# Linear attention and a mixture of experts on one core: the first chunk's scores and the list entries get other places in the issue order

## The chip, the cores and the metric

The kernel runs on one core of a Trainium2 chip. The metric is the device time of one execution in microseconds; three runs are known of the kernel before. A profile of one further execution shows what each engine did. The engines go by short names: PE is TensorE's matmuls and PEld its weight loads, DVE is VectorE, ACT is ScalarE, POOL is GpSimd, SP is the engine that here only issues transfers.

## What is computed

Input `x` is 2048 tokens of 512 numbers. The block is a pre-norm layer of two parts, all in float32:

```
x = x + attention(layernorm(x))
x = x + experts(layernorm(x))

attention: q = x Wq (16 heads of 128), k = x Wk, v = x Wv (4 heads of 128, each shared by 4 q heads)
           rotary embedding on q and k, then f(t) = elu(t) + 1
           state_t = state_{t-1} + k_t v_t^T,  z_t = z_{t-1} + k_t
           out_t = (q_t state_t) / (q_t z_t + 1e-6);  out Wo

experts:   scores = softmax(x Wc) over 64; the best 8 of scores + bias
           32 of the 64 are experts with weights (silu(x Wg) * (x Wu)) Wd; the others add no output
           of their own but scale the token's sum; at most 256 tokens to an expert
```

The recurrence over tokens is computed in chunks of 128: inside a chunk as masked scores times values, across chunks through the state.

## The kernel before

The tokens go in four blocks (`sb`, 512 tokens), each of four chunks (`c`, 128 tokens); there are four key heads (`g`), each with four query heads (`R`). The loop over blocks is at L552, over heads at L556, over chunks at L571.

For each block, `norm_block` (L267) normalises the tokens and puts them, transposed, into `xT`, of which there is one buffer. `values` (L288) makes `va`, the values of a chunk for all heads. `project` (L313) makes `kT` and `qT` of one head: one PSUM tile `pk` and four `pq` (tag `pj`, two buffers), each of four float32 matmuls that the profile shows as two instructions each, followed by `rope_feature` (L300), which is six operations on VectorE and one exponential on ScalarE per tile. `kT` and `qT` have two buffers, so a head's projection can write its result only when the attention of the head before last has ended.

`attend` (L332) handles one chunk of one head: the scores `psc` (L338; PSUM pool `p_sc`, one buffer), the masked scores `at` on VectorE (L340, two buffers), the products `po` of the masked scores with the values (L347) and of the queries with the state (L350), the denominators `den` (L353, L354), the divided rows `osb` on ScalarE (L356), the new state (L359 to L369), and the transposed result `oT` (L372, L373).

In the order of the program the projection of the next head (L560), or for the last head the next block's norm and first projection (L562, L563), stands ahead of the attention of the present one (L572).

After the last head's chunk `c` the result of chunk `c - 1` goes through `output` (L375): 16 products with `wo` into `px`, the residual sum `x1` (L387), and the second layer norm, whose power (the reciprocal square root) runs on GpSimd (`lnr`, L264) and whose normalised row is `xw` (L395). The function `rstd_of` keeps the power traced last as `rstd_of.last`. Chunks wait in the list `waiting` for `route` (L398), which scores the experts, takes the best 8, and makes `ai`, the places of a chunk's tokens in the lists of the experts. `list_further` (L197) then issues eight indirect transfers on GpSimd (L200), one for each of a token's eight choices, into `slots` in DRAM. `route_and_list` (L487) is the two together.

In the last block, `rows_so_far` (L514) reads the first rows of the lists back through SP (`idx_8b`, L518) and reduces them on VectorE to `low` (L520); `rows_in_groups` (L525) makes of them the index `idx_m_f`, which is used at L656, ahead of the first gathers of the experts' phase. Chunk 14's routing is issued between the two halves of chunk 15's output, and its list behind chunk 15's power.

The instructions are not issued in the order of the program text alone. A planner at compile time gives every instruction the priority of its place in the text and orders each engine's queue by priority among those that it reckons ready, with buffers given out as they come free. On the chip each queue then runs in that fixed order. `tc.issue_after(ins)` makes the instructions in its block that run on the engine of `ins` come behind `ins` in that engine's queue. The dependences between tiles are kept by semaphores.

The experts' phase (L829 on) gathers rows, runs the experts in groups of four, and adds to the output by indirect transfers; the change leaves it as it is.

Of the kernel before, what the change touches and what calls it, by code (L numbers as in the profile page):

```python
# [18 lines left out]
P = 128  # L19
# [48 lines left out]
def linattn_moe(  # L68
# [128 lines left out]
    def list_further(ch, ai, ks=range(TOPK)):  # L197

        for k in ks:
            one = nc.gpsimd.indirect_dma_start(  # L200
                out=slots[k][:, :],
                out_offset=bass.IndirectOffsetOnAxis(ap=ai[:, k : k + 1], axis=0),
                in_=tok[:, ch : ch + 1],
                in_offset=None,
                bounds_check=NS - 1,
                oob_is_err=False,
            )
        return one


    with ExitStack() as ph:
# [47 lines left out]
        def rstd_of(var, n, name):  # L259

            v = sml.tile([P, n], F32, tag=f"lnv{n}", name=f"lnv_{name}")
            nc.vector.tensor_scalar(v, var, 1e-5, None, ALU.add)
            r = sml.tile([P, n], F32, tag=f"lnr{n}", name=f"lnr_{name}")
            rstd_of.last = nc.gpsimd.tensor_tensor(r, v, mhalf[:, :n], ALU.pow)  # L264
            return r
# [63 lines left out]

        state = [None] * G  # L330

        def attend(sb, g, c, proj, va, oT):  # L332

            kT, qT = proj
            n = f"{sb}_{g}_{c}"
            cc = ts(c, P)
            psc = p_sc.tile([P, R, P], F32, tag="sc", name=f"psc_{n}")
            nc.tensor.matmul(psc, lhsT=kT[:, cc], rhs=qT[:, :, cc], start=True, stop=True)  # L338
            at = tmp.tile([P, R, P], F32, tag="at", name=f"at_{n}")
            nc.vector.tensor_tensor(at, psc, causal.unsqueeze(1).to_broadcast([P, R, P]), ALU.mult)  # L340
            old = state[g]
            osb = tmp.tile([P, R, HD], F32, tag="osb", name=f"osb_{n}")
            for j in range(R // 2):
                po = p_o.tile([P, 2, HD + 1], F32, tag="o", name=f"po_{n}_{j}")
                for i in range(2):
                    r = 2 * j + i
                    nc.tensor.matmul(po[:, i, :], lhsT=at[:, r, :], rhs=va[:, g, :],  # L347
                                     start=True, stop=(old is None))
                    if old is not None:
                        nc.tensor.matmul(po[:, i, :], lhsT=qT[:, r, cc], rhs=old,  # L350
                                         start=False, stop=True)
                den = sml.tile([P, 2], F32, tag="den", name=f"den_{n}_{j}")
                nc.vector.tensor_scalar(den, po[:, :, HD], 1e-6, None, ALU.add)  # L353
                nc.vector.reciprocal(den, den)  # L354
                for i in range(2):
                    nc.scalar.mul(osb[:, 2 * j + i, :], po[:, i, :HD], den[:, i : i + 1])  # L356
            if sb < NSB - 1 or c < NC - 1:
                pk = p_tr.tile([P, HD], F32, tag="tr", name=f"pk_{n}")
                nc.tensor.transpose(pk, kT[:, cc], ident)  # L359
                kk = tmp.tile([P, HD], F32, tag="kk", name=f"kk_{n}")  # L360
                nc.scalar.copy(kk, pk)
                pst = p_ms.tile([P, HD + 1], F32, tag="ms", name=f"pst_{n}")
                nc.tensor.matmul(pst, lhsT=kk, rhs=va[:, g, :], start=True, stop=True)  # L363
                new = stp.tile([P, HD + 1], F32, tag=f"st{g}", name=f"state_{n}")
                if old is None:
                    nc.vector.tensor_copy(new, pst)  # L366
                else:
                    nc.vector.tensor_tensor(new, pst, old, ALU.add)
                state[g] = new  # L369
            pt = p_tr.tile([P, R, P], F32, tag="tr", name=f"pot_{n}")  # L370
            for r in range(R):
                nc.tensor.transpose(pt[:, r, :], osb[:, r, :], ident)  # L372
            nc.vector.tensor_copy(oT[:, :, cc], pt)  # L373

        def output(sb, c, oTs, between=None):  # L375

            ch = sb * NC + c
            xs, _, _ = blocks[sb]
            px = p_pj.tile([P, D], F32, tag="pj", name=f"px_{ch}")
            for h in range(H):  # L380
                if between is not None and h == H // 2:
                    between()
                output.last = nc.tensor.matmul(px, lhsT=oTs[h // R][:, h % R, ts(c, P)],  # L383
                                                  rhs=wo[h // R][:, h % R, :],
                                                  start=(h == 0), stop=(h == H - 1))
            x1 = tmp.tile([P, D], F32, tag="row", name=f"x1_{ch}")
            nc.vector.tensor_tensor(x1, px, xs[:, c, :], ALU.add)  # L387
            tc.chain_iter_dep("out", nc.scalar.dma_start(out=out[ts(ch, P), :], in_=x1).ins)
            st = sml.tile([P, 6], F32, tag="st", name=f"st2_{ch}")
            nc.vector.bn_stats(st, x1)  # L390
            mv = sml.tile([P, 2], F32, tag="mv", name=f"mv2_{ch}")
            nc.vector.bn_aggr(mv, st)
            rstd = rstd_of(mv[:, 1:2], 1, f"2_{ch}")
            xw = tmp.tile([P, XW], F32, tag="xw", name=f"xw_{ch}")
            nc.vector.tensor_scalar(xw[:, :D], x1, mv[:, 0:1], rstd, ALU.subtract, ALU.mult)  # L395
            return xw
# [90 lines left out]
        def route_and_list(ch, xw):  # L487
            list_further(*route(ch, xw))
# [60 lines left out]
        projs = {(0, 0): project(0, 0, xTs[0])}  # L549
        oTs = {}  # L550
        waiting = []
        for sb in range(NSB):  # L552
            last = sb == NSB - 1
            if not last:
                blocks[sb + 1] = load_block(sb + 1)
            for g in range(G):  # L556
                if g == 0:
                    vas = [values(sb, c, xTs[sb]) for c in range(NC)]
                if g + 1 < G:
                    projs[sb, g + 1] = project(sb, g + 1, xTs[sb])  # L560
                elif not last:
                    xTs[sb + 1] = norm_block(sb + 1)  # L562
                    projs[sb + 1, 0] = project(sb + 1, 0, xTs[sb + 1])  # L563
                if last and g == 1:
                    rank_e = place()
                if last and g == G - 1:
                    for i in range(2):
                        load_pair(i)
                oT = otp.tile([P, R, SB], F32, tag="oT", name=f"oT_{sb}_{g}")
                oTs[sb, g] = oT  # L570
                for c in range(NC):  # L571
                    attend(sb, g, c, projs[sb, g], vas[c], oT)  # L572
                    if g == G - 1:
                        if c != 1 and waiting:
                            route_and_list(*waiting.pop(0))
                        if c >= 1:
                            waiting.append((sb * NC + c - 1,
                                            output(sb, c - 1, [oTs[sb, i] for i in range(G)])))
            listed = []
            if last:  # L580
                low_f = rows_so_far()
            xw = output(sb, NC - 1, [oTs[sb, i] for i in range(G)],
                        (lambda: listed.append(route(*waiting.pop(0)))) if last else None)
            with tc.issue_after(rstd_of.last.ins):
                for one in listed:
                    list_further(*one)
            while waiting:
                route_and_list(*waiting.pop(0))
            if last:
                with tc.issue_after(output.last.ins):  # L590
                    rows_in_groups(low_f)
                route(sb * NC + NC - 1, xw)
            else:
                waiting.append((sb * NC + NC - 1, xw))
# [43 lines left out]
    _, words = nc.values_load_multi_w_load_instructions(  # L638
        flags[0:1, :], min_val=0, max_val=65535,
        skip_runtime_bounds_check_because="a sum of 16 different powers of two below 2^16",  # L640
    )
# [189 lines left out]
    one = list_further(S // P - 1, ai_last, range(HEAD))  # L831
    with tc.issue_after(one.ins):
        for q in range(EARLY):
            g = gather(xg_b[q], idx_b[:, q : q + 1], XR)
# [3 lines left out]
    with tc.issue_after(g.ins):  # L838
        one = list_further(S // P - 1, ai_last, range(HEAD, TOPK))
# [23 lines left out]
    def gather_first(q):  # L863
        gather(xg_o[q % 2], column(Q * q, 0), S)
        return gather(xg_t[q % 2], column(Q * q, 1), S)
# [39 lines left out]
    for q in range(NQ):  # L905
        g = gather_first(q + 1) if q + 1 < NQ else None
# [63 lines left out]
```

## Time and profile before

| what | value |
|---|---|
| median of three runs (lowest, highest) | 1131.75 us (1129.96, 1133.35) |
| the profiled execution: time, span | 1135.13 us, 1133.4 us |
| mean granted TensorE clock in the span | 0.964 |
| 0 to 100 us: TensorE, VectorE busy | 89.3, 70.8 us |
| 100 to 200 us | 93.2, 66.7 |
| 200 to 300 us | 98.2, 52.4 |
| 300 to 400 us | 93.1, 77.5 |
| 400 to 500 us | 98.6, 46.4 |
| 500 to 600 us | 93.4, 72.5 |
| 600 to 700 us | 98.1, 42.9 |
| 700 to 800 us | 98.6, 79.1 |
| 800 to 900 us | 83.6, 44.2 |
| 900 to 1000 us | 77.8, 26.1 |
| 1000 to 1134 us | 102.0, 28.5 |

The blocks of attention begin near 20, 244, 463 and 682 us; the stretches with fewer transfers and more VectorE work are the projections and the attention of the heads, those with TensorE near 98 are mostly the outputs. Attention ends near 900 us, and the experts' phase follows.

A row of a timeline holds the start, the duration, the engine, the line, the operation, the tiles written and read, the size, the number of instructions merged into it, and in brackets how long the engine stood idle before it and what ended that. A row of the waits names who waited for whom, with the total in us, how often, and the longest. In the windows view each engine has its busy time and, in brackets, its instructions, and then come the granted clock, the share of the transfer engines and GB/s. Matmuls overlap, so that the busy time of PE is an upper bound of its work.

### The profile page before, as it was taken

The page shows a single profiled execution, that of the slowest core. Times are in us where ns is not written, and L with a number is a line of the kernel's source. Part 1 is how long each engine was busy: PE and PEld are TensorE (multiplying, and loading weights), DVE is VectorE, ACT ScalarE, POOL GpSimd, SP SyncE. Part 2 cuts the span into 40 slices and gives each one's busy share as a digit, 9 for nine tenths or more (in the row PEclk, how much of TensorE's full clock was granted, in tenths as well). Part 3 has the DMA queues.
Part 4 walks back from the last instruction along what each step waited for, and adds up shares of the span by engine and source line. Part 5 has one row for each costly group of instructions (what it writes and reads, how often), then busy time and mean ns, then how long its engine had stood idle before and what let it go on. Part 6 is the DMA issues. An engine that isn't in the chain of part 4 may idle for free.

```text
span 1133.4 us, 12755 instructions
## 1 busy us (share of the span) xinstructions
PE 1025.8 (91%) x4420; PEld 583.2 (51%) x4420; DVE 607.0 (54%) x1661; ACT 208.5 (18%) x541; POOL 230.3 (20%) x290
## 2 busy tenths in 40 slices
PE   6999899999998999999899999999988477999980
PEld 3455455444655554455465544555654234665650
DVE  4778864446786743388847324778523522222220
ACT  1123221001223210122232001222201110111110
POOL 6000000432000035300001432000142543222332
PEclk9999999999999999999999999999989678999995
DMA  9400000010000000100000000023002297999310
GB/s 352 157 1 1 19 1 10 30 66 1 1 1 19 1 30 29 57 1 1 1 1 11 29 20 20 1 93 131 20 20 88 92 359 253 307 363 382 80 22 13
DMA packets 51806, 87.26 MB, mean 77 GB/s; under 512 B 11342, under 2 KB 11470, under 8 KB 51728
## 3 DMA queue, kind: packets, MB, share of 16 engines
q1 hardware_dynamic: 35248, 67.31, 16.1%
q0 software_dynamic: 10720, 10.08, 4.0%
q10 hardware_dynamic: 5760, 8.92, 2.1%
q8 instruction: 38, 0.62, 0.2%
q14 instruction: 40, 0.33, 0.1%
HBM read 75.92 MB, written 15.88 MB: 81 GB/s over the span
## 4 chain that ended last, share of the span: by engine, by line
PE 55%; DVE 25%; issue 9%; DMA 5%; ACT 2%; POOL 1%; SPq 0%; ACTq 0%; POOLq 0%; DVEq 0%
PE px L383 16%; PE pq L325 5%; PE pu L797 4%; PE po L347 4%; PE psc L338 4%; DVE rb_q L306 3%; DVE rb_q L307 3%; DMA out_dram<-y,idx 3%; PE po L350 3%; PE pot L372 3%; DVE qT L308 3%; PE pv L293 3%; DVE qT L305 3%; DVE qT L311 3%; PE pk L318 2%
## 5 line engine op out<-in xcount | busy, mean ns | idle before, releaser
L383 PE MATMUL px<-wo,oT 128*128 128x512 f32 x512 | 231.7, 597 | 0.0
L325 PE MATMUL pq<-xT,wq 128*128 128x512 f32 x512 | 230.5, 595 | 0.5 <-DVE rb_q L307 0.4
L200 POOL DMA_INDIRECT slots<-tok,ai x120 | 117.9, 982 | 242.0 <-DVE ai L484 209.7
L325 PEld LDWEIGHTS pq<-xT,wq 128*128 128x128 f32 x512 | 93.4, 191 | 106.6 <-issue 91.8
L383 PEld LDWEIGHTS px<-wo,oT 128*128 128x128 f32 x512 | 93.8, 192 | 97.8 <-issue 97.8
L347 PE MATMUL po<-va,at 128*128 128x129 f32 x512 | 99.5, 280 | 12.1 <-DVE at L340 11.7
L356 ACT ACTIVATE osb<-po,den 128x128 f32<-128x128 f32 x256 | 77.8, 365 | 152.1 <-DVE den L354 99.4
L347 PEld LDWEIGHTS po<-va,at 128*128 128x128 f32 x512 | 80.3, 194 | 35.7 <-DVE at L340 21.9
L350 PE MATMUL po<-state,qT 128*128 128x129 f32 x480 | 93.9, 278 | 0.0
L296 POOL MEMSET va<- 128x4 f32 x16 | 1.5, 111 | 415.5 <-PE pst L363 415.5
L350 PEld LDWEIGHTS po<-state,qT 128*128 128x128 f32 x480 | 73.7, 194 | 1.3 <-DVE state L366 0.8
L372 PE MATMUL pot<-ident,osb 128*128 128x128 f32 x256 | 60.5, 301 | 14.8 <-ACT osb L356 13.7
L310 ACT ACTIVATE rb_q<-rb_q 128x512 f32<-128x512 f32 x64 | 40.3, 630 | 179.2 <-DVE rb_q L309 164.0
L387 DVE TENSOR_TENSOR x<-px,xs 128x512 f32<-128x512 f32 x16 | 11.1, 692 | 109.1 <-PE px L383 74.3
L372 PEld LDWEIGHTS pot<-ident,osb 128*128 128x128 f32 x256 | 35.9, 145 | 62.8 <-ACT osb L356 49.9
L338 PE MATMUL psc<-qT,kT 128*128 128x512 f32 x128 | 68.0, 614 | 0.0
L797 PE MATMUL pu<-xeT,gu 128*128 128x224 f32 (+1 forms) x352 | 63.8, 341 | 4.1 <-DVE xeT L740 3.4
L797 PEld LDWEIGHTS pu<-xeT,gu 128*128 128x128 f32 x352 | 60.4, 195 | 6.3 <-ACT y L821 2.3
L318 PE MATMUL pk<-xT,wk 128*128 128x512 f32 x128 | 61.0, 613 | 0.8 <-ACT xT L285 0.7
L340 DVE TENSOR_TENSOR at<-psc,causal 128x512 f32<-128x512 f32 x64 | 43.9, 687 | 32.0 <-PE psc L338 31.8
L373 DVE COPY oT<-pot 128x512 f32<-128x512 f32 x64 | 43.9, 686 | 25.7 <-PE pot L372 25.5
L293 PE MATMUL pv<-wv,xT 128*128 128x512 f32 x128 | 57.0, 595 | 0.0
(222 smaller groups left out, 1193.2 us busy)
## 6 DMA issues: line engine op xcount, KB each, us to landing
gu<-in_wgu_dram SPq DMA_DIRECT2D x32, 1024.0 KB
dn<-in_wdn_dram SPq DMA_DIRECT2D x32, 512.0 KB
rows<-xw ACTq DMA_DIRECT2D x16, 272.0 KB
wq<-in_wqT_dram SPq DMA_DIRECT2D x4, 1024.0 KB
wo<-in_woT_dram SPq DMA_DIRECT2D x4, 1024.0 KB
out_dram<-x ACTq DMA_DIRECT2D x16, 256.0 KB
xs<-in_x_dram SPq DMA_DIRECT2D x3, 1024.0 KB
slots<-tok,ai POOLq DMA_INDIRECT x120
```

The source lines that it names most:

```text
L200: one = nc.gpsimd.indirect_dma_start(out=slots[k][:, :], out_offset=bass.IndirectOffsetOnAxis(ap=ai[:, k : k + 1], axis=0), in_=tok[:, ch ...
L293: nc.tensor.matmul(pvf, lhsT=xT[:, k, ts(c, P)], rhs=wv[:, k, :], start=(k == 0), stop=(k == KD - 1))
L318: nc.tensor.matmul(pk, lhsT=wk[:, k, ts(g, HD)], rhs=xT[:, k, :], start=(k == 0), stop=(k == KD - 1))
L325: nc.tensor.matmul(pq, lhsT=wq[g][:, k, ts(r, HD)], rhs=xT[:, k, :], start=(k == 0), stop=(k == KD - 1))
L338: nc.tensor.matmul(psc, lhsT=kT[:, cc], rhs=qT[:, :, cc], start=True, stop=True)
L340: nc.vector.tensor_tensor(at, psc, causal.unsqueeze(1).to_broadcast([P, R, P]), ALU.mult)
L347: nc.tensor.matmul(po[:, i, :], lhsT=at[:, r, :], rhs=va[:, g, :], start=True, stop=(old is None))
L350: nc.tensor.matmul(po[:, i, :], lhsT=qT[:, r, cc], rhs=old, start=False, stop=True)
L356: nc.scalar.mul(osb[:, 2 * j + i, :], po[:, i, :HD], den[:, i : i + 1])
L372: nc.tensor.transpose(pt[:, r, :], osb[:, r, :], ident)
L383: output.last = nc.tensor.matmul(px, lhsT=oTs[h // R][:, h % R, ts(c, P)], rhs=wo[h // R][:, h % R, :], start=(h == 0), stop=(h == H - 1))
L797: nc.tensor.matmul(pu[:, a, :m], lhsT=weights[e][0][:, k, a, c, :], rhs=xeT[:, k, :m], start=(k == 0), stop=(k == KD - 1))
```

## The change

The scores and the mask leave `attend` for a function of their own, `scores`. For a head's chunk 0 it is called at the start of the head, ahead of the values (for g = 0) and of the next head's projection or the next block's norm; for the other chunks it is called right before `attend`, as before. In the last head of a block, `route` and `list_further` are parted: the entries of a chunk routed in this round are issued on GpSimd after `output` of the same round is traced, and behind the power traced last.

```diff
-        def attend(sb, g, c, proj, va, oT):
+        def scores(sb, g, c, proj):
             kT, qT = proj
...
             nc.tensor.matmul(psc, lhsT=kT[:, cc], rhs=qT[:, :, cc], start=True, stop=True)
             at = tmp.tile([P, R, P], F32, tag="at", name=f"at_{n}")
             nc.vector.tensor_tensor(at, psc, causal.unsqueeze(1).to_broadcast([P, R, P]), ALU.mult)
+            return at
+
+        def attend(sb, g, c, proj, at, va, oT):
+
+            kT, qT = proj
+            n = f"{sb}_{g}_{c}"
+            cc = ts(c, P)
             old = state[g]
...
             for g in range(G):
+                at = scores(sb, g, 0, projs[sb, g])
                 if g == 0:
                     vas = [values(sb, c, xTs[sb]) for c in range(NC)]
                 if g + 1 < G:
...
                 for c in range(NC):
-                    attend(sb, g, c, projs[sb, g], vas[c], oT)
+                    if c:
+                        at = scores(sb, g, c, projs[sb, g])
+                    attend(sb, g, c, projs[sb, g], at, vas[c], oT)
                     if g == G - 1:
+                        entries = []
                         if c != 1 and waiting:
-                            route_and_list(*waiting.pop(0))
+                            entries.append(route(*waiting.pop(0)))
                         if c >= 1:
                             waiting.append((sb * NC + c - 1,
                                             output(sb, c - 1, [oTs[sb, i] for i in range(G)])))
+                        with tc.issue_after(rstd_of.last.ins):
+                            for one in entries:
+                                list_further(*one)
```

At c = 0 no output is traced in the round, so the power traced last is an earlier one: the next block's norm, or in the last block chunk 11's. At c = 2 it is the power of the block's chunk 1, at c = 3 that of its chunk 2.

## The prediction

> **What bounds the kernel now.** I read the page's busy times first, then the windows by stage, then the waits, then timelines of the stretches that the waits point to.
>
> ```profile
> PE 1025.8 (91%) x4420; PEld 583.2 (51%) x4420; DVE 607.0 (54%) x1661; ACT 208.5 (18%) x541; POOL 230.3 (20%) x290
> ```
>
> TensorE is busy for 91% of the span. From 60 to 857 us, where attention runs, the windows view gives TensorE 763.7 us of 797 and VectorE 495.0. TensorE's queue sets the end there, so an edit is worth the waits that it takes from that queue or adds to it. The waits view names those that the change touches:
>
> ```profile
> DVE xw L395 <- POOL lnr L264: 22.6, 12, 5.5
> PEld po L347 <- DVE at L340: 21.9, 24, 3.5
> PE po L347 <- DVE at L340: 11.7, 8, 3.3
> ```
>
> Columns: total us, times, longest. PE and PEld stand at the same places, so the two po rows are not added. The 3.3 us case recurs at the head g = 2 of blocks 0, 1 and 2. TensorE's timeline in block 1:
>
> ```profile
> 331.64 11.32 PE L325 MATMUL pq<-xT,wq 128*128 128x512 f32 x26
> 342.80 1.02 PE L338 MATMUL psc<-qT,kT 128*128 128x512 f32 x2
> ...
> 347.99 0.49 PE L347 MATMUL po<-va,at 128*128 128x129 f32 x2 [3.21 <-DVE at L340]
> ...
> 350.40 1.91 PE L338 MATMUL psc<-qT,kT 128*128 128x512 f32 x2
> ...
> 353.69 0.39 PE L347 MATMUL po<-va,at 128*128 128x129 f32 x2
> ```
>
> The projection of head 3 (pq) runs dense; only then come the scores of head 2's first chunk, and TensorE stands 3.21 us for the masked scores `at`. Blocks 0 and 2 show 3.31 (at 133.61) and 3.21 (at 566.92). Why `at` is late stands on VectorE:
>
> ```profile
> 346.65 0.68 DVE L308 TENSOR_TENSOR qT<-qT,rb_q 128x512 f32<-128x512 f32 x1
> 347.25 0.68 DVE L340 TENSOR_TENSOR at<-psc,causal 128x512 f32<-128x512 f32 x1
> ...
> 349.02 0.69 DVE L311 SCALAR_TENSOR_TENSOR qT<-qT,rb_q 128x512 f32<-128x512 f32 x1 [0.56 <-ACT rb_q L310]
> ```
>
> The scores were out at 343.8, but VectorE was still busy with the rotations of head 3 and took `at` in a gap of them. A second loss follows. In the windows the column after POOL is the granted clock:
>
> ```profile
> 349.30:352.70 3.40, 3.40 (x12) 2.26 (x11) 1.32 (x6) 1.25 (x4) 0.00 (x0) 0.50 0.00 0
> ```
>
> After each of the three waits the clock is 0.50 for 3.4 us, which costs about 1.7 us of a busy TensorE.
>
> The lists show on GpSimd and VectorE (chunk 13):
>
> ```profile
> 848.15 0.97 POOL L200 DMA_INDIRECT slots<-tok,ai  x1 [0.31 <-issue]
> 849.15 0.58 POOL L264 TENSOR_TENSOR lnr<-lnv,mhalf 128x1 f32<-128x1 f32 x1
> ```
> ```profile
> 847.68 0.15 DVE L262 TENSOR_SCALAR lnv<-mv 128x1 f32<-128x1 f32 x1
> 849.76 0.55 DVE L395 TENSOR_SCALAR xw<-x,mv,lnr 128x512 f32<-128x512 f32 x1 [1.92 <-POOL lnr L264]
> ```
>
> The power for the norm was ready to run at 847.83 and ran behind eight list entries at 849.15; VectorE stood at `xw` for it, and with it den, osb and the transposes on TensorE (1.24 us idle at 851.11).
>
> **Part 1, the scores.** Nothing is added. For 16 heads two score matmuls (0.43 us apart) and one `at` (0.69 us) go ahead of the next projection, and no DMA goes with them. The planner orders each engine by priority and readiness; psc has one PSUM buffer, so head 2's first scores can run when `at` of head 1's last chunk is done (326.7 in block 1), long before 342.8.
>
> Heads g = 2, blocks 0 to 2: at most 3.21 + 1.7 = 4.9 us each. The second chunk's `at` still needs a gap in the rotations, which end at 349.7: with it at 349.7 the next po starts at 350.5 instead of 353.69, 3.2 us; if 342.8 to 350.5 then holds an idle stretch that again halves the clock, 1.5. Between 1.5 and 4.9 I take 4.0, near the upper end, because a gap was open at 347.25 and the second `at` can have it: 3 x 4.0 = **12.0 us** (4.5 to 14.7).
>
> Heads g = 0: TensorE waits 0.36 us each at 69.53, 282.40, 501.34 and 719.46 behind eight matmuls of the next key. Up to 1.4 us; I take **1.0**. Heads g = 1 and 3 show no such wait, or have one inside other work: 0. The earlier `at` shifts the rotations by 0.69 us; TensorE covers that with a second PSUM buffer whose slack I read as 0.4 to 0.8 us (L307 of the first query ends 335.1, the third query's matmuls begin at about 335.9). I price that at 0, and in the last rival at its full size.
>
> **Part 2, the lists.** Only chunks 0 and 1 of each block get a new place: 8 lists of 8 issues go behind the power of the chunk after them. At c = 0 the last traced power belongs to work long done, so lists 3, 7 and 11 stay, and with list 11 the longest wait (5.49 us at 826.86). The powers of chunks 1, 5, 9 and 13 come free: TensorE's idle at L372 was 0.85, 0.90, 0.94 and 1.24, together 3.9; at chunks 2, 6 and 10 VectorE waited 2.2 to 2.4 us but TensorE had output matmuls and stood nowhere: 0. Some of the 3.9 belongs to the power's own 0.57 us; I take **3.5** (0 to 3.9).
>
> What now queues behind a list on GpSimd: a `va` memset (214.62, block 0), about 10 us later, first needed when ACT copies values from 248.57 on; and the power of the chunk after. A list takes 10.2 us; chunk 9's would start at about 670 and end near 680, chunk 11's power comes at 683.26, so 3 us to spare. Without that cover VectorE would stand as it does now.
>
> **Part 3, the end of attention.** List 13 feeds `low`, and that goes the wrong way:
>
> ```profile
> 866.58 0.69 DVE L390 BATCH_NORM_STATS2 st<-x 128x6 f32<-128x512 f32 x1
> 872.24 0.57 DVE L520 TENSOR_REDUCE low<-idx_8b 32x32 int32<-32x256 int32 x1 [4.97 <-DMA idx_8b<-slots]
> 872.74 0.16 DVE L392 BATCH_NORM_AGGREGATE mv<-st 128x2 f32<-128x6 f32 x1
> ```
>
> VectorE stands 4.97 us at `low`: the planner took it for ready 5 us too early, and TensorE idled 1.85 us for chunk 14's `xw` (874.53). List 13 ran from 859.45 and `low` started 12.8 us after it. Behind the power of chunk 14, whose st ends at 867.27, it starts at about 868.4, so `low` can run at 881.2. SP's eight reads of the entries move as well, 9 us, and behind them the loads of weight pair 2 (SP at 871.43, four DMAs); their experts are used by group 1, after 970, and pair 3 only starts at 908, so they hide. The index built from `low` is next needed at 899.19: hidden too.
>
> But `low` stands in VectorE's fixed order. `mv` must now precede it, so `xw` of chunk 14 comes 5.4 us earlier and the 1.85 us go. If the planner is 5 us too early again, `low` sits near 876, among the routing of chunk 14, and `here`, which TensorE waits for, stands until 881.2. Bounds: -1.9 (the order is right) to +7 (`low` directly behind `xw`: 10 us of stand, less 3 us that the last output's matmuls cover). I take +5.0 less 1.9, **+3**, since 4.97 is the planner's error in this row.
>
> **Sum:** -12.0 - 1.0 - 3.5 + 3 = **-13.5 us** on this execution: span 1133.4 becomes 1119.9, its time of 1135.13 (1.7 around the span) becomes 1121.6. The median of the runs is 3.4 below that execution; 1131.75 - 13.5 = **1118**.
>
> **Rivals.**
> (a) The shortened wait still halves the clock, 3 x 1.7 = 5.1 back: **1123**. For it: 3.2 us of idle did so each time. Against: the 1.85 us wait did not, the clock is 1.00 from 834.0 to 888.6. [...]
> (b) `low` at its worst: +7 and one more slow stretch of 1.7 in place of +3, 1118 + 5.7 = **1124**. For it: the wait of 4.97. Against: `low` has `mv` in front of it now.
> (c) The planner puts the scores where they were, as TensorE is never free for them: only part 2 and 3 remain, -0.5: **1131**. Against: they get priority over pq, not spare time.
> (d) Slower. VectorE paces the projection: `at` ahead of the rotations pushes each by 0.69 us, and 12 heads with a next projection behind them give TensorE 12 x 0.69 = 8.3 us of waits for a free pq buffer, while head 2's second `at` waits as the first did. With -3.5 + 3 this gives +7.8: **1139**. It decides as soon as the slack of that buffer is below 0.69; one reading was 0.4. Against: po of the first chunk can now fill such gaps.
>
> **How the numbers follow.** Forecast 0.48, (a) 0.12, (b) 0.16, (c) 0.08, (d) 0.16. A difference under 0.3% (3.4 us) can't be told from none here. Faster 0.76, same 0.08, slower 0.16. The bounds of the parts sum to -14.7 - 1.4 - 3.9 - 1.9 = -21.9, or 1110. I give 1109 to 1137, which leaves out most of (d) and little else; the forecast's own range is 1110 to 1124.
>
> **What would show it.** Right: no wait over 2 us at po <- `at`, no 0.50 clock near 134, 349 and 568, psc of g = 2 before the last pq; the waits of `xw` on lnr near 0.8 us except after list 11; `low` with a wait of about 5 us behind `xw` of chunk 14. Wrong: pq waiting for rb_q L307 several us in all, the 3.2 us stall moved to the second chunk, or the last output ending over 7 us later relative to `px` of chunk 14.

## The result, and the profile after

| | before | after |
|---|---|---|
| median of 13 runs each, us (lowest, highest) | 1131.75 (1128.04, 1136.02) | 1123.16 (1118.7, 1129.45) |
| ratio, with its interval | | 0.9925 (0.9907 to 0.9942) |
| the profiled execution: time, span, us | 1135.13, 1133.4 | 1119.89, 1118.2 |
| last product `px` of attention ends, us | 884.4 | 871.9 |
| first gather of the experts' phase starts, us | 902.9 | 893.0 |

The change makes the kernel 8.6 us faster. The two profiled executions differ by 15 us: some 5 of these arise in the last transfers of the experts' phase, which the change leaves alone, so the parts are read from the stages and the size from the runs. From the first gather to the end the phase takes 230.5 us before and 225.2 after; over all 14 profiles of this study it varies from 224.0 to 232.4 us.

The busy times of the page hardly move; only the span does:

```profile
span 1118.2 us, 12738 instructions
PE 1025.2 (92%) x4420; PEld 582.2 (52%) x4420; DVE 606.0 (54%) x1661; ACT 206.5 (18%) x541; POOL 231.3 (21%) x290
```

The waits (total us, times, longest):

```profile
PEld pot L379 <- ACT osb L363: 48.6, 88, 3.8
...
PE pot L379 <- ACT osb L363: 15.8, 18, 3.6
DVE xw L402 <- POOL lnr L264: 14.5, 16, 3.7
...
PEld po L354 <- DVE at L340: 5.7, 19, 0.5
```

TensorE no longer stands for the masked scores: its weight loads waited 21.9 us for `at`, now 5.7 and never over 0.5. VectorE's waits for the power fell from 22.6 to 14.5 us. With the one after list 11 (3.74) left out, each of them is now 0.5 to 0.8 us. But the wait of `pot`, the transposes of the divided rows `osb`, grew from 13.7 to 15.8 us in all, though its longest, 4.5 us behind list 11, fell to 2.7: the 3.6 us are at a new place. TensorE and VectorE at the head g = 2 of block 1, the place that the prediction showed, with the duration second and the wait in brackets:

```profile
330.55 1.02 PE L338 MATMUL psc<-qT,kT 128*128 128x512 f32 x2
...
333.14 12.18 PE L325 MATMUL pq<-xT,wq 128*128 128x512 f32 x28
...
345.16 0.39 PE L354 MATMUL po<-va,at 128*128 128x129 f32 x2
...
347.48 0.69 DVE L307 TENSOR_TENSOR rb_q<-pq,sn 64x512 f32<-64x512 f32 x1
...
348.81 0.68 DVE L308 TENSOR_TENSOR qT<-qT,rb_q 128x512 f32<-128x512 f32 x1
349.41 0.15 DVE L360 TENSOR_SCALAR den<-po 128x2 f32<-128x2 f32 x1
...
350.58 1.13 ACT L363 ACTIVATE osb<-po,den 128x128 f32<-128x128 f32 x4
...
350.99 0.33 PE L379 MATMUL pot<-ident,osb 128*128 128x128 f32 x1 [2.69 <-ACT osb L363]
...
351.41 0.40 PE L354 MATMUL po<-va,at 128*128 128x129 f32 x2
```

The first half went as meant: the scores are out at 330.55, and `po` starts in the moment that the projection ends, at 345.16. Its last product is out at 347.1. Then the denominators `den` need a gap in the same rotations of the next head, and get it at 349.41. TensorE stands 2.69 us for `osb`, and the second chunk's `po` starts at 351.41. Times of the two profiles are best compared from the start of the block, since block 1 begins at 243.85 before and at 245.72 after: the first `po` comes 4.7 us earlier in the block, the second one 4.1. Block 2 shows the same 2.69 at 566.58, block 0 3.57 at 135.64.

The lengths of the four blocks (first `pv` to the next block's first `pv`, the last one to its last `px`), and from there to the first gather, in us, from one profile each:

| kernel | block 0 | 1 | 2 | 3 | last `px` to first gather |
|---|---|---|---|---|---|
| before | 210.5 | 219.0 | 218.7 | 202.8 | 18.5 |
| scores alone | 213.0 | 217.8 | 216.6 | 197.8 | 18.8 |
| lists alone | 210.3 | 218.9 | 218.7 | 201.5 | 21.1 |
| lists alone but list 13 | 209.5 | 217.7 | 217.7 | 205.6 | 17.8 |
| after | 212.1 | 215.3 | 215.6 | 195.3 | 21.1 |
| one query ahead of each chunk (best) | 204.3 | 208.3 | 208.5 | 187.8 | 19.6 |

### The profile page after: what moved, and what is told of

Read it like the earlier page. It is cut to its first block, busy times and chain, and to the rows that moved or that the text cites. A ratio compares the mean times of both kernels' runs of the same rounds, so it can differ in the third digit from the quotient of the medians.

```text
span 1118.2 us, 12738 instructions
## 1 busy us (share of the span) xinstructions
PE 1025.2 (92%) x4420; PEld 582.2 (52%) x4420; DVE 606.0 (54%) x1661; ACT 206.5 (18%) x541; POOL 231.3 (21%) x290
## 4 chain that ended last, share of the span: by engine, by line
PE 49%; DVE 22%; issue 18%; DMA 5%; POOL 2%; ACT 2%; ACTq 0%; SPq 0%; POOLq 0%; DVEq 0%
PE px L390 17%; PE pu L811 4%; PE pq L325 4%; DMA out_dram<-y,idx 3%; PE pot L379 3%; DVE rb_q L306 3%; DVE rb_q L307 3%; DVE qT L308 3%; PE psc L338 3%; PE po L354 3%; DVE qT L305 3%; DVE qT L311 3%; PE po L357 2%; PE py L826 2%; PE pu_b L767 2%
## 5 line engine op out<-in xcount | busy, mean ns | idle before, releaser
L325 PE MATMUL pq<-xT,wq 128*128 128x512 f32 x512 | 227.9, 594 | 3.1 <-DVE rb_k L307 2.1
L379 PE MATMUL pot<-ident,osb 128*128 128x128 f32 x256 | 62.3, 302 | 17.2 <-ACT osb L363 15.8
```

Of the source, the lines that this page charges most:

```text
L325: nc.tensor.matmul(pq, lhsT=wq[g][:, k, ts(r, HD)], rhs=xT[:, k, :], start=(k == 0), stop=(k == KD - 1))
```

## The experiments

Twelve kernels, each against runs of the kernel before on the same chip. Changes in us are (ratio - 1) x 1131.75.

| kernel | ratio (interval) | change |
|---|---|---|
| 1 scores alone | 0.9955 (0.9933 to 0.9977) | -5.1 |
| 2 lists alone | 1.0001 (0.9981 to 1.0021) | 0.1 |
| 3 after, list 13 at once | 0.9904 (0.9872 to 0.9936) | -10.9 |
| 4 after, lists of c = 0 behind the power too | 0.9895 (0.9869 to 0.9921) | -11.9 |
| 5 after, projection spread over the chunks | 0.9758 (0.9735 to 0.9781) | -27.4 |
| 6 after, `low` behind the routing | 0.9914 (0.9886 to 0.9942) | -9.7 |
| 7 after, lists 2 and 6 behind the block norm's power | 0.9928 (0.9905 to 0.9951) | -8.1 |
| 8 edits 4 to 7 together | 0.9687 (0.966 to 0.9713) | -35.4 |
| 9 lists alone but list 13 | 1.0018 (0.9996 to 1.004) | 2.0 |
| 10 after again | 0.991 (0.9891 to 0.9929) | -10.2 |
| 11 as 8, one query ahead of each chunk | 0.9654 (0.9629 to 0.9679) | -39.2 |
| 12 as 11, lists as before | 0.972 (0.9687 to 0.9753) | -31.7 |

### 1 and 2: each half of the change alone

The first kernel has `scores` and the call ahead of the projection, with `route_and_list` as before; the second has the lists' edit, with `attend` as before.

> The scores go ahead, the lists stay as before. Theory A (the head starts gave most of the 8.6 us, as forecast with 13 us for them): ratio to before about 0.992, 9 us faster. Theory B (the wait at a head's start only moved from `at` to `den` and `osb` behind the rotations, and waits for a free pq buffer came in at g = 0; the lists gave most): 0.997 to 1.000, at most 3 us faster, with the wait for osb of 2.8 us at g = 2 of blocks 1 and 2 still there and the long wait behind list 11 in the last block near 4.5 us with a half clock after it.

> The lists go behind the power, the scores stay. Theory A: 0.998, 2 us faster (3.5 for four transposes, less what `low` takes at the end). Theory B: 0.994 to 0.995, 6 us faster, of which more than half in the last block. In both the waits of `at` of 3.2 us at g = 2 of blocks 0 to 2 stay, with a half clock of 3.4 us after each.

The scores alone give 5.1 us, the lists alone nothing that can be measured. Neither theory holds whole: the waits that theory B names for the scores are there (2.68 us for `osb` in blocks 1 and 2, 1.07 us for a projection buffer at g = 0), but the lists did not give the rest. The wait of `xw` after list 11 (longest row: 5.5 before, 3.8 with the scores alone, 5.5 with the lists alone) shrank with the scores, which the prediction had not foreseen. The lists did what they were meant to: TensorE's waits at the transposes behind the powers of chunks 1, 5, 9 and 13 (0.85, 0.90, 0.94 and 1.24 us) are gone in the second kernel, and stand as before in the first (0.83, 0.92, 0.92, 1.23). What the lists cost at the end shows on TensorE and VectorE of the second kernel:

```profile
864.86 0.55 DVE L395 TENSOR_SCALAR xw<-x,mv,lnr 128x512 f32<-128x512 f32 x1 [0.76 <-POOL lnr L264]
...
879.07 0.57 DVE L520 TENSOR_REDUCE low<-idx_8b 32x32 int32<-32x256 int32 x1 [3.38 <-DMA idx_8b<-slots]
...
880.24 0.28 PE L451 MATMUL pf<-ident,free 128*32 128x128 f32 x1 [3.00 <-DVE free L449]
```

List 13 goes behind the power of chunk 14, `low` comes 14.2 us behind `xw`, and TensorE stands 3.00 us in the routing that is queued behind it. From the last `px` to the first gather it takes 2.5 us more.

### 3, 6 and 9: the end of attention

The third kernel and the ninth issue list 13 right after its routing (in the changed kernel, and in the lists alone):

```diff
-                            entries.append(route(*waiting.pop(0)))
+                            one = route(*waiting.pop(0))
+                            if last and c == NC - 1:
+                                list_further(*one)
+                            else:
+                                entries.append(one)
```

The sixth keeps the lists and moves `low` behind the routing of chunk 14 on VectorE (`lowest` is L527 to L529 of `rows_so_far`, `route.last` the instruction that makes `ai`):

```diff
-                low_f = rows_so_far()
+                idx_8b = rows_so_far()
...
+            if last:
+                with tc.issue_after(route.last.ins):
+                    low_f = lowest(idx_8b)
```

> The changed kernel, but list 13 is issued right after its routing, ahead of chunk 14's power. If list 13 behind the power costs the end of attention 3 us (forecast), this is 2 to 3 us faster than the changed kernel: 0.990 to before. If VectorE's stand at `low` costs nothing net, or the power then waits for the list as before, it equals the changed kernel: 0.9925.

> The changed kernel with `low` behind the routing of chunk 14 on VectorE. If `low` standing among that routing costs TensorE its 2.7 us idle ahead of pf and more behind it, the stretch from the last output's end to the first gather falls from 21.1 to about 18.5 us or the output ends 2.5 us earlier: 0.990 to before. If the reads of the lists are the bound, `low` only waits elsewhere: 0.9925.

> The kernel before with the list entries of every chunk but list 13 issued behind the next power; the scores stay where they were, and list 13 is issued right after its routing. If the lists alone brought nothing because list 13's new place costs the end 2.5 us, this is 0.997 to 0.998 of before (2.5 to 3.5 us faster). If the lists' places give nothing within attention either, it is 1.000.

None can be told from the kernel that it changes. In the profile of the third the end takes 18.9 us again, but the wait is back inside attention: VectorE stands for `low`, and TensorE for `xw` behind it:

```profile
864.95 0.57 DVE L527 TENSOR_REDUCE low<-idx_8b 32x32 int32<-32x256 int32 x1 [5.90 <-DMA idx_8b<-slots]
...
867.24 0.63 PE L409 MATMUL prt<-ident,xw 128*128 128x128 f32 x4 [2.78 <-DVE xw L402]
```

So list 13's place moves 2 to 4 us from one side of the last `px` to the other. The ninth kernel refutes that it is what made the lists alone worthless: its first three blocks are 1.0, 1.3 and 1.0 us shorter than before, its last is 2.8 longer, and its runs are no faster. In the second kernel the same edit of these three blocks shows only 0.2, 0.1 and 0.0: its profile has 6.8 us of half clock at each of the three waits for `at`, that of the ninth 3.4, as before (mean clocks of the two profiles 0.956 and 0.968). In the sixth, `low` stands at 872.7 behind the routing, yet the way to the first gather stays 20.9. That suggests that behind a list this late the chain of list, read-back, `low` and index sets that time; no run parts it further.

### 4 and 7: the lists that still stood ahead of a power

Kernel 4 keeps a list of c = 0 (3, 7, 11) for the round after; kernel 7 puts lists 2 and 6 behind the power of the next block's norm.

```diff
-                        entries = []
+                        if c == 0:
+                            entries = []
...
-                        with tc.issue_after(rstd_of.last.ins):
-                            for one in entries:
-                                list_further(*one)
+                        if c:
+                            with tc.issue_after(rstd_of.last.ins):
+                                for one in entries:
+                                    list_further(*one)
+                            entries = []
```
```diff
                     xTs[sb + 1] = norm_block(sb + 1)
+                    with tc.issue_after(rstd_of.last.ins):
+                        while behind_norm:
+                            list_further(*behind_norm.pop())
...
-                route_and_list(*waiting.pop(0))
+                one = route(*waiting.pop(0))
+                if sb + 2 < NSB:
+                    behind_norm.append(one)
+                else:
+                    list_further(*one)
```

> The changed kernel, but the list of a block's first routed chunk (3, 7, 11) also waits for the power of the next round. If the remaining 2.7 us idle of TensorE at chunk 12's power are list 11's alone, it is 2.5 us faster than the changed kernel (0.990 to before), and the wait of xw on lnr there falls from 3.7 to 0.8 us. If the lists then pile up behind each other and make `low` later, it is 0.9925 or slower.

> The changed kernel with lists 2 and 6 behind the power of the next block's norm. The stand of VectorE of 8.8 to 10.3 us at xn goes. If the waits for a free pq buffer at g = 0 of blocks 1 and 2 (2.0 us each) come from that stand, they go and the kernel is 3 to 4 us faster than the changed one: 0.989 to 0.990 to before. If they come from the early `at`, they stay: 0.9925.

In kernel 4 the wait of `xw` after list 11 falls to 0.8 us, as expected, TensorE's 2.7 us there are gone, and the last block takes 192.8 us (195.3 and 196.9 in the two profiles of the changed kernel); the runs gain 3.4 us at most on it, within the intervals. Kernel 7 answers to a loss that the change brought with it. The changed kernel in block 1, head g = 0:

```profile
265.18 1.00 DVE L279 TENSOR_SCALAR xn<-xs,mv,lnr 128x512 f32<-128x512 f32 x2 [10.32 <-issue]
...
268.25 3.70 PE L325 MATMUL pq<-xT,wq 128*128 128x512 f32 x8 [1.04 <-DVE rb_k L307]
...
272.23 3.70 PE L325 MATMUL pq<-xT,wq 128*128 128x512 f32 x8 [0.28 <-DVE rb_q L307]
```

VectorE stands 10.32 us at `xn`, the next block's normalised rows. The view names no releaser, but on GpSimd the power that `xn` reads ran at 264.10, right behind list 2, which had been issued from 254.14 on. The rotations of the key are queued behind `xn`, and TensorE waits for a free projection buffer. With list 2 behind that power the same projection of kernel 7 is one dense row:

```profile
263.40 13.98 PE L325 MATMUL pq<-xT,wq 128*128 128x512 f32 x32
```

So these waits do come from list 2. But the scores are needed too: the kernel before has the stand at `xn` (8.8 us) and next to no wait of the projection (0.2 us in each of blocks 1 and 2), and kernel 1, with its lists as before, has the 1.07 us. And the 3 to 4 us expected did not come: in that profile the clock fell after the `pot` waits of all three blocks (0.50 from 349.26 to 352.67 us and from 564.30 to 567.71, and 0.8 in the page's slice from 113 to 141), and the mean clock of its six runs was 0.9605, against 0.9648 for the kernel before beside it.

### 5, 8 and 11: the projection spread over the chunks

If VectorE gives the rotations of the next head the gaps that `den` and `at` need, the cure is to have fewer rotations there at once. Kernel 5 puts only the key and the first query of the next head ahead of the head's chunks, query 1 ahead of chunk 1, queries 2 and 3 ahead of chunk 2. Kernel 11 has one query ahead of each of the chunks 1, 2 and 3.

```diff
-        def project(sb, g, xT):
+        def project(sb, g, xT, whole=True):
...
-            for r in range(R):
+            queries(sb, g, xT, qT, range(R if whole else 1))
+            return kT, qT
+
+        def queries(sb, g, xT, qT, rs):
+
+            for r in rs:
...
-                    projs[sb, g + 1] = project(sb, g + 1, xTs[sb])
+                    projs[sb, g + 1] = project(sb, g + 1, xTs[sb], False)
...
+                    if g + 1 < G and c in (1, 2):
+                        queries(sb, g + 1, xTs[sb], projs[sb, g + 1][1], (1,) if c == 1 else (2, 3))
```

> The changed kernel, but for g = 0, 1, 2 only the key and the first query of the next head's projection stand ahead of the chunks; the second query stands ahead of chunk 1, the third and fourth ahead of chunk 2. If the wait for osb of 2.8 us at g = 2 (3.7 in block 0) is there because `den` queues behind the rotations, it falls below 1 us, the half clocks at 134 and 568 us go with it, and the kernel is 8 to 12 us faster than the changed one (0.982 to 0.986 to before). If that wait is TensorE having nothing to do whatever VectorE's order is, it comes back at chunk 1, 2 or 3 and the ratio stays 0.9925.

> All together, and the list of a block's first routed chunk behind the next power as well. If the gains add up: 0.975 to 0.980 to before. If a wait that is removed in one place comes back in the next: 0.985 to 0.989.

> The version with all four edits, but the projections of the next head's queries stand one ahead of each of chunks 1, 2 and 3, in place of query 1 ahead of chunk 1 and queries 2 and 3 ahead of chunk 2. If the third one's rotations are still done by the time the next head's first scores need them, 0.967 to 0.969 of before, the same as the version with all four or 1 to 2 us faster. If the next head's first scores then wait for the rotations, 0.972.

Kernel 5 in block 1, TensorE and VectorE around two chunks of the head g = 2:

```profile
336.62 1.02 PE L342 MATMUL psc<-qT,kT 128*128 128x512 f32 x2
337.06 0.16 DVE L364 TENSOR_SCALAR den<-po 128x2 f32<-128x2 f32 x1
...
337.70 1.02 PE L330 MATMUL pq<-xT,wq 128*128 128x512 f32 x2
...
338.56 0.43 PE L383 MATMUL pot<-ident,osb 128*128 128x128 f32 x2
...
339.91 5.32 PE L330 MATMUL pq<-xT,wq 128*128 128x512 f32 x12
...
349.35 0.33 PE L383 MATMUL pot<-ident,osb 128*128 128x128 f32 x1 [1.15 <-ACT osb L367]
```

`den` now runs 0.4 us after the last `po` ends (2.3 in the changed kernel), and TensorE fills the time to `osb` with projection. Where two queries stand together the wait is 1.15; with one ahead of each chunk (kernel 11) the longest wait for `osb` is 0.7 and that of `xw` for the power 0.8 (the latter by the lists' edits that it also has):

```profile
DVE xw L406 <- POOL lnr L264: 11.5, 16, 0.8
...
PE pot L383 <- ACT osb L367: 7.5, 22, 0.7
```

With 1090.88 us in the median of its runs, beside 1130.14 for the kernel before, kernel 11 beats both kernels of this study: 39 us, over four times what the change brought. Kernel 5 gained 19 us on the changed kernel where at most 12 were expected, and kernel 8 beat its forecast too (0.9687, at best 0.975 expected): in kernel 5 all four blocks are 3.5 to 6.2 us shorter than after the change, not only the heads g = 2. The spread does two things at once, it leaves `den` and `at` gaps among the rotations and gives TensorE work for the wait, and no run parts the two. Whether its split is better than that of kernel 8 is not settled: the two intervals overlap.

### 10 and 12: do the halves add?

Kernel 10 is the changed kernel once more; kernel 12 is kernel 11 with every list back to where it was (`list_further(*route(...))` at once).

> The changed kernel once more, beside the other two. If its first figure stands, 0.9925 again, 8 to 9 us faster, more than the scores alone (5.1) and the lists alone (0) add up to. If those add, it is 0.9955 (5 us faster) here, and the first figure was too good.

> The version with one query ahead of each chunk, and every list entry of a chunk issued right after its routing again, as in the kernel before (the last block's final list stays behind its power). Theory: the lists' places save VectorE and TensorE time (span times mean clock was 3.3 us lower with the lists alone), which the kernel before gave back as a lower clock. Where no half clock follows the head's scores, nothing is given back: undoing the lists' places costs those 3.3 us and the 8 us by which the version with all four edits beat the spread alone, together some 11: 0.975 of before. Rival: the lists' places are worth nothing by themselves: 0.965, as with them.

Kernel 10 gives -10.2 us, so the first figure was not too good. The halves alone add up to -5.0 (+-3.4 from their intervals), the two measurements of the whole have a mean of -9.3 (+-1.5): the lists are worth more with the scores than without, by 4.3 us (+-3.7), which is not far beyond the noise. In kernel 12 the lists' places are worth 0.972 - 0.9654, or 7.5 us (intervals added in squares: 2.8 to 12). That excludes the rival, that they are worth nothing, and can't be told from the 11 us of the theory. It is no second measurement of the same thing: kernel 12 takes back 13 lists, kernel 2 moved 8 (the other five are 3, 7 and 11 of kernel 4 and 2 and 6 of kernel 7). In its profile VectorE waits 23.4 us for the power at `xw` again and 23.1 at `xn` (4.6 in kernel 11), and attention's last `px` ends 8.5 us later.

## Why the prediction was right, and where it was off

The sign and the range held, and so did the first step of the mechanism: the scores go ahead, and the wait for the first `at` is gone. The forecast of -13.5 was 4.9 us too much, and that it was no further off is in part luck. For the first three blocks the terms add up to about -15 us (-12, three quarters of -1 and some 2.4 of the 3.5); the blocks became 5.2 us shorter in the first profile and 3.8 in the second. For the last block and the way to the first gather they add up to about +1.7; there 4.9 and 3.4 us were gained, for a reason that the prediction did not have.

**Heads g = 2, -12.0: mis-sized, and this is the term that the difference comes from.** "A gap was open at 347.25 and the second `at` can have it" was the step that failed. The first `at` did leave the path, but what TensorE met next was not the second `at`: it was `pot` of the first chunk, whose `den` waits for the same gaps in the rotations. The waits of 3.31, 3.21 and 3.21 us in blocks 0, 1 and 2 became 3.57, 2.69 and 2.69. TensorE's lost time in the 22 us from 128, 343 and 561 us on (from one matmul's start to the next, less the spacing that dense rows have, 0.43 us for a float32 pass of 512 and 0.11 us for 128, so that a slow clock counts too) was 8.2, 8.7 and 8.3 us before and is 8.6, 5.4 and 5.7 after (8.5, 5.4 and 6.9 in the second profile): -5.5, or -4.4, in place of -12. Block 1 came near the 4.0 that were forecast for each, block 0 gave nothing. Kernel 5 shows that `den` waits for the rotations: with fewer of them there it runs 0.4 us behind the last `po`, in place of 2.3.

**Rival (a), the clock,** holds in part. Block 0 stayed at half clock for 6.8 us in place of 3.4; blocks 1 and 2 kept full speed in the first profile of the changed kernel, and in the second one block 2 did not. The time of this rival, 1123, is what was measured, but that is chance: it takes the waits for as short as the forecast has them and the clock for halved after each, and the runs show longer waits and a clock that is halved in some blocks only. That a shortened wait keeps full speed was the author's estimate, with the one wait of 1.85 us for it; at 2.69 us it held in some profiles and not in others.

**Heads g = 0, -1.0: wrong in sign.** The four waits of 0.36 us are gone, 1.4 us in all. But in blocks 1 and 2 the changed kernel waits 1.5 us for projection buffers (1.04 + 0.28 + 0.20 in the brackets of the timeline of block 1); before, there was one such wait of 0.2 in each. Kernel 7 shows the cause, `xn` behind list 2, together with the earlier scores.

**Lists, -3.5, and the end, +3:** the sum of -0.5 agrees with what kernel 2 gave (0.1, interval -2.2 to 2.4). The waits of the first term (3.9 us) did go, 1.0 to 1.3 us per block in kernel 9, and the end takes 2.5 us more. `low` landed where the prediction put it, among the routing of chunk 14, but it did not stand for about 5 us: 1.21 us in the changed kernel, 3.38 with the lists alone. What cost time was the routing behind it, `free` and `here`, for which TensorE waited 2.66 and 1.86 us:

```profile
855.69 0.55 DVE L402 TENSOR_SCALAR xw<-x,mv,lnr 128x512 f32<-128x512 f32 x1 [0.75 <-POOL lnr L264]
855.85 1.30 POOL L200 DMA_INDIRECT slots<-tok,ai  x1 [0.19 <-issue]
...
869.56 0.57 DVE L527 TENSOR_REDUCE low<-idx_8b 32x32 int32<-32x256 int32 x1 [1.21 <-DMA idx_8b<-slots]
...
870.74 0.28 PE L458 MATMUL pf<-ident,free 128*32 128x128 f32 x1 [2.66 <-DVE free L456]
...
874.22 0.27 PE L473 MATMUL ph<-tok,here 128*128 128x2 bf16 x4 [1.86 <-DVE here L469]
```

List 13 to `low` is 13.7 us, where the prediction had 12.8.

**Not foreseen:** the wait after list 11, which "stays", fell from 5.49 to 3.74 us (3.77 with the scores alone), TensorE's behind it from 4.47 to 2.72, and of the 6.8 us of half clock that followed (827.17 to 834.00) none was left in the first profile (1.00 from 815.5 to 826.0), 3.4 us in the second. The last block gained 5.0 us by the scores and 7.5 by both (5.9 in the second profile). That made good part of the first term; why the scores shorten this wait was not followed up.

**Rival (d)** fell: the projections wait 3.1 us in all for buffers (0.4 before), not 8.3, and all of it in the two projections behind `xn`. **Rival (c)** fell at once: the scores do stand ahead.

Open: why the halves give less apart than together, and how much of that is the clock. The profile of the lists alone has seven times 3.4 us at half clock in attention, that of the kernel before five and of the changed kernel two and, in the second profile, four; the mean clock of the 12 runs of the lists alone is 0.9593, against 0.9622 in the 23 runs beside it. Kernel 9 shows the same (0.9621 against 0.9652). That speaks for the clock taking the lists' gain back, but no run held the clock fixed. And the spread of the experts' phase from profile to profile, 8 us, is larger than the difference in question, so that single profiles can't settle it.

## What to carry to other kernels

When a wait is taken away, look at what comes next on the same queue and needs the same busy engine: here `den` needed the same gap in the rotations as `at` did. Work that is only a supply (the next head's projection) did better here between the steps of the dependent chain, in pieces, than ahead of it as one dense run: it fills the chain's waits and leaves the other engines room (the longest wait of TensorE for `osb` is 0.7 us in kernel 11, 3.6 in the changed kernel). And a queue that is served in order, as GpSimd's (in the changed kernel the power that `xn` reads ran at 264.10, behind list 2, issued from 254.14 on), should have its short urgent instruction ahead of its long batch, but what the batch feeds then comes later by that much.

## What the runs showed of the hardware

In the profile of the kernel before, the waits of 3.31, 3.21 and 3.21 us for `at` were each followed by 3.4 us at 0.50, the 4.47 us behind list 11 by 6.8; in the first profile of the changed kernel the 3.57 us of block 0 were followed by 6.8. After 1.85 us in the kernel before (for chunk 14's `xw`, at 874.53) and after the 2.72 us behind list 11 in the first profile of the changed kernel (at 819.11) the clock stayed at 1.00. The waits of 2.69 us at the heads g = 2 went both ways: in the first profile of the changed kernel those of blocks 1 and 2 were followed by full speed, in the second one that of block 2 was followed by half clock. Block 2 in the two profiles, in three stretches of 3.4 us each (busy us of PE, PEld, DVE, ACT and POOL, then the granted clock):

```profile
561.27:564.68 3.41, 2.62 (x18) 1.95 (x17) 3.33 (x7) 0.78 (x2) 0.00 (x0) 1.00 0.00 0
564.68:568.10 3.42, 1.52 (x13) 1.46 (x14) 2.67 (x10) 1.82 (x6) 0.00 (x0) 1.00 0.02 5
568.10:571.51 3.41, 3.00 (x20) 2.10 (x19) 2.15 (x8) 1.52 (x5) 0.00 (x0) 1.00 0.00 0
```

and in the second profile (kernel 10):

```profile
560.88:564.29 3.41, 2.73 (x19) 2.05 (x18) 3.33 (x7) 0.78 (x2) 0.00 (x0) 1.00 0.00 0
564.29:567.70 3.41, 1.41 (x12) 1.36 (x13) 2.66 (x10) 1.82 (x6) 0.00 (x0) 1.00 0.02 5
567.70:571.12 3.42, 3.42 (x15) 2.94 (x14) 1.49 (x6) 1.25 (x4) 0.00 (x0) 0.50 0.00 0
```

The wait ends in the middle stretch of both. TensorE was busy for 1.52 and 1.41 us of it, the modelled ends of its matmuls counted in; the next stretch ran at 1.00 in one profile and at 0.50 in the other. In kernel 12 a stretch whose longest wait was 1.10 us (262.44 to 265.85, TensorE busy for 1.86) was followed by one at 0.50. Kernels 5, 8 and 11, whose longest waits for `osb` were 1.15, 1.1 and 0.7 us, have no half clock in attention at all; the mean clocks of their profiles are 0.973, 0.971 and 0.971, against 0.964 for the kernel before. So the length of a wait alone did not tell here whether half clock follows it; what else decides was not shown, as no run changed the length or the place of one wait alone.
